# Causal attention of a decoder layer: the turn of the exponentials moved from TensorE to VectorE squares and a trip through DRAM

## The chip, the cores and the metric

The kernel runs on one core of a Trainium2 chip. All data are float32. The metric is the device time of one launch in microseconds (us); lower is better.

The core has five engines that each work through a queue of their own, in order: TensorE (PE: matmuls and transposes, results into PSUM), VectorE (DVE), ScalarE (ACT), GpSimd (POOL) and SyncE (SP), which here issues the DMAs. An engine that has to wait holds back all that is queued behind the waiting instruction.

## The reference

A decoder of two layers on x of shape [8, 128, 512] and a context of the same shape. Layer 0: causal self-attention with 32 heads of 16, an autocorrelation mixer against the context, a mixture of low-rank experts. Layer 1: causal attention with distance bias, cross-attention, low-rank experts. Each of the six blocks is followed by a residual addition and a layer norm. The change touches the first block alone:

```python
q = (x @ Wq.T + bq).reshape(b, l, h, hd).transpose(0, 2, 1, 3)      # k, v alike
scores = jnp.einsum('bhqd,bhkd->bhqk', q, k) / math.sqrt(hd)
scores = jnp.where(causal, scores, -jnp.inf)
att = jax.nn.softmax(scores, axis=-1)
out = jnp.einsum('bhqk,bhkd->bhqd', att, v)
out = out.transpose(0, 2, 1, 3).reshape(b, l, d)
return out @ Wo.T + bo
x = _layernorm(x + attention(x))
```

## The kernel before, in words

The batch is taken in pairs of sequences p = 0..3. For each pair there are four steps f = 0..3, and a step handles 8 heads of both sequences: 16 steps n = 0..15 in all (loop at L513). Where a step number stands in brackets below, it is that step's tile.

One step is an object of class `Heads16` (L146). Its work, in order:

- Scores (L165): 32 small matmuls into two PSUM tiles of two banks each. Rows are queries, columns are keys: per head pair r = 0..3, 384 columns, which are the keys of two heads for the late half of the queries (256 columns) and for the early half (128 columns).
- `causal_bias` (L369): VectorE adds the mask and writes tile `e`, [128, 4, 384], in two halves. Tile `e` has two buffers.
- Maxima (L182): four VectorE reductions.
- `exps` (L194): 16 ScalarE activations in two halves of 8, each with its sum, in place on `e`.
- `turn` (L210): VectorE takes the reciprocals `rc` of the sums (L215), GpSimd spreads them to 256 columns in `rb` (L218), TensorE transposes the 12 blocks of `e` (L225) and the two of `rb` (L233) into PSUM, VectorE and ScalarE copy the halves of `e` out to `pT` (L226), ScalarE copies the reciprocals to `rT` (L235).
- `out` (L237): 48 small matmuls of the values with `pT` (L244, L250), and one VectorE multiplication by `rT` into `oT` (L258).

The steps are staggered by the loop. In step n it issues: scores, bias, maxima and the first half of the exponentials of step n; `out` of step n-2; the queries and keys of step n+1 (L350: eight matmuls `pq` and `pk`, `qT` copied by ScalarE at L354, `kbd` made by VectorE at L358); `turn` of step n-1; pieces of the autocorrelation block (`auto`, L532 and L541, from step 7 on, for the first two pairs); values (L347) or output projections with their norms (`projection`, L371; residual addition L103) in some steps; the second half of the exponentials of step n.

That is the order in which the program is written. A scheduling layer then fixes each engine's own order when the program is built, so an instruction may stand earlier or later on its queue than the source has it. Buffers are taken from pools: a tile's next user waits until the last reader of that buffer is done. The score tiles and the transposes share one PSUM pool of two tiles (`ps2`), so the scores of a step and the transposes of another wait for each other's copies.

The weights, tokens and context are loaded at the start by some 30 DMAs on SP's queue (L300 to L338), 14 MB up to 40 us; a few later loads stand behind them.

In the last block (cross-attention, L917) the kernel already turns exponentials by VectorE in squares of 32 by 32 (`nc.vector.transpose`, L958) and moves the squares with small DMAs from SBUF to SBUF (L964). The class `Heads16` also serves the fourth block (layer 1), where the division is done ahead of the turn; that use is as it was after the change.

Of the kernel before, what the change touches and what calls it, by code (L numbers as in the profile page):

```python
# [11 lines left out]
F32 = mybir.dt.float32  # L12
AF = mybir.ActivationFunctionType
ALU = mybir.AluOpType
AX = mybir.AxisListType
PSUM = bass.MemoryType.PSUM

P = 128
B, S, D = 8, 128, 512
NC = D // P  # L20
H, HD = 32, 16
# [17 lines left out]
def bc(ap, shape):  # L39
    return ap.to_broadcast(shape)  # L40
# [3 lines left out]
def decoder(ctx: ExitStack, tc: tile.TileContext, a: dict, out: bass.AP):  # L44
    nc = tc.nc
# [4 lines left out]
    sm = ctx.enter_context(tc.tile_pool(name="sm", bufs=4))  # L50
# [28 lines left out]
    causal = masks[:, C_CAUSAL : C_CAUSAL + 3 * P]  # L79
# [66 lines left out]
    class Heads16:  # L146
# [11 lines left out]
        def __init__(self, pool, units, bias, o_dst, name, between=()):  # L158
            self.pool, self.units, self.o_dst, self.name, self.rc = pool, units, o_dst, name, None
            s = [banks(f"s_{name}_{i}") for i in range(2)]  # L160
            for part, cols, keys in ((0, slice(0, 2 * P), P), (1, slice(2 * P, 3 * P), 64)):
                for r in range(4):
                    rows = slice(32 * r, 32 * r + 32)
                    for u, (qT, kbd, _, _) in enumerate(units):
                        nc.tensor.matmul(  # L165
                            s[r // 2][64 * u : 64 * u + 64, r % 2, cols],
                            lhsT=qT[rows, 64 - 64 * part : P - 64 * part], rhs=kbd[rows, :, :keys],
                            start=True, stop=True,
                        )
            self.e = pool.tile([P, 4, self.W], F32, tag="e", name=f"e_{name}", bufs=2)  # L170
            self.m = sm.tile([P, 2, 4, 2], F32, tag="m", name=f"m_{name}")
            self.su = sm.tile([P, 2, 4, 2], F32, tag="su_a", name=f"su_{name}")
            for i in range(2):
                rs = slice(2 * i, 2 * i + 2)
                self.scored = bias(self.e[:, rs, :], s[i][:, :, : self.W], rs)

                while i and between:
                    with tc.issue_after(self.scored.ins):
                        self.scored = between.pop(0)()
                with tc.issue_after(self.scored.ins):  # L180
                    for part in range(2):
                        self.scored = nc.vector.tensor_reduce(  # L182
                            self.m[:, part, rs, :], self.by_heads(part)[:, rs], AX.X, ALU.max, negate=True
                        )

        def by_heads(self, part):
            return self.e[:, :, 2 * P * part : 2 * P + P * part].rearrange("p r (x k) -> p r x k", x=2)
# [22 lines left out]
        def turn(self):  # L210


            if self.rc is None:
                rc = sm.tile([P, 16], F32, tag="rc", name=f"rc_{self.name}")
                nc.vector.reciprocal(rc, self.su.rearrange("p a r x -> p (a r x)"))  # L215

                rb = self.pool.tile([P, 2, 8, HD], F32, tag="rb", name=f"rb_{self.name}", bufs=1)
                nc.gpsimd.tensor_copy(rb, bc(rc.rearrange("p (a h) -> p a h", a=2).unsqueeze(3), [P, 2, 8, HD]))  # L218
            self.pT = self.pool.tile([P, 4, self.W], F32, tag="pT", name=f"pT_{self.name}", bufs=1)
            for i in range(2):  # L220
                pt = banks(f"pt_{self.name}_{i}")
                for r in range(2):
                    for k in range(3):
                        cols = slice(k * P, (k + 1) * P)
                        nc.tensor.transpose(pt[:, r, cols], self.e[:, 2 * i + r, cols], ident)  # L225
                (nc.scalar.copy if i else nc.vector.tensor_copy)(  # L226
                    self.pT[:, 2 * i : 2 * i + 2, :], pt[:, :, : self.W]
                )
            if self.rc is not None:
                return  # L230
            pr = bank(f"pr_{self.name}")
            for a in range(2):
                nc.tensor.transpose(pr[:, a * P : (a + 1) * P], rb[:, a].rearrange("p h d -> p (h d)"), ident)  # L233
            self.rT = self.pool.tile([P, 2, P], F32, tag="rT", name=f"rT_{self.name}", bufs=1)
            nc.scalar.copy(self.rT, pr[:, : 2 * P].rearrange("p (a q) -> p a q", a=2))  # L235

        def out(self):  # L237
            o = bank(f"o_{self.name}")
            for u, (_, _, v, vd) in enumerate(self.units):
                v, vd = (t() if callable(t) else t for t in (v, vd))  # L240
                late = slice(u * P + 64, u * P + P)
                for x in range(2):
                    for r in range(4):
                        nc.tensor.matmul(  # L244
                            o[32 * r : 32 * r + 32, late],
                            lhsT=v[:, 48 * r + 16 * x : 48 * r + 16 * x + 32],
                            rhs=self.pT[:, r, x * P + 64 * u : x * P + 64 * u + 64], start=(x == 0), stop=(x == 1),
                        )
                for r in range(4):
                    nc.tensor.matmul(  # L250
                        o[32 * r : 32 * r + 32, u * P : u * P + 64],
                        lhsT=vd[:, 32 * r : 32 * r + 32],
                        rhs=self.pT[:, r, 2 * P + 64 * u : 2 * P + 64 * u + 64], start=True, stop=True,
                    )
            if self.rc is not None:
                nc.vector.tensor_copy(self.o_dst, o[:, : 2 * P].rearrange("p (u q) -> p u q", u=2))
                return
            nc.vector.tensor_tensor(  # L258
                self.o_dst.rearrange("p u (a q) -> p u a q", a=2),
                o[:, : 2 * P].rearrange("p (u a q) -> p u a q", u=2, a=2),  # L260
                self.rT[:, ::-1].rearrange("p a (u q) -> p u a q", u=2),
                ALU.mult,
            )

# [20 lines left out]
    ap = attn.enter_context(stage("a0", 2))  # L285
# [1 line left out]
    bq4 = ap.tile([P, NC], F32, tag="bq4", name="bq4", bufs=1)  # L287
    dft = cp.tile([P, N_DFT], F32, tag="dft", name="dft")

    idle = ap.tile([P, 4, 3 * P], F32, tag="e", name="idle").rearrange("p r k -> p (r k)")[:, :512]  # L290
    nc.vector.memset(idle, 0.0)
    nobody = bank("nobody")
    for _ in range(2):
# [56 lines left out]
    def queries_keys(p, f):  # L350
# [14 lines left out]
        )  # L365
        return qT, kbd

    def causal_bias(e, s, r0):
        return nc.vector.tensor_tensor(e, s, bc(causal.unsqueeze(1), [P, 2, 3 * P]), ALU.add)  # L369

    def projection(b, oT):  # L371
        po = bank(f"po0_{b}")
# [121 lines left out]
    steps = [(p, f) for p in range(NP) for f in range(NC)]  # L494
# [12 lines left out]
    oTs = []  # L507
# [5 lines left out]
    for n, (p, f) in enumerate(steps):  # L513
        if f == 0:
            oTs.append(ap.tile([P, 2, NC, P], F32, tag="oT", name=f"oT0_{p}"))
        qT, kbd = qk
        units = []
        for j in range(2):
            toks = slice(j * P, (j + 1) * P)
            of = lambda i, w, p=p, f=f, j=j: vs[p, j][i].rearrange("p a x d -> p (a x d)")[:, f * w : (f + 1) * w]  # L520
            units.append((qT[:, toks], kbd[:, :, toks], lambda of=of: of(0, 192), lambda of=of: of(1, 128)))
        now = Heads16(ap, units, causal_bias, oTs[p][:, :, f, :], f"a0_{p}_{f}")
        now.exps(0)
        catch_up(now.scored)

        if turned:
            turned.out()
        if n + 1 < len(steps):
            qk = queries_keys(*steps[n + 1])
        if prev:  # L530
            prev.turn()
        auto(n, 0)  # L532

        for made in values_at.get(n, ()):
            values(*made)
        now.exps(1)
        if 0 < f < 3 and p:
            projection(2 * p - 3 + f, oTs[p - 1])
        if f == 1 and p and p + 1 < NP:
            xts.append(tokens(p + 1))  # L540
        auto(n, 1)  # L541
        if n >= begun and f == NC - 1:
            context(n // NC)
        turned, prev = prev, now
# [222 lines left out]
    ap = layer.enter_context(stage("a1", 2))  # L767
# [18 lines left out]
    class Front:  # L786
# [27 lines left out]
        def begin(self):  # L814
            self.kT = cross[1].tile([P, NS, 2, 2 * P], F32, tag="kT", name=f"kTx_{self.pr}")
            self.qT = cross[1].tile([P, NX, 2 * P], F32, tag="qT", name=f"qTx_{self.pr}")
# [27 lines left out]
    for b in range(B):  # L844
# [3 lines left out]
        for f in (0, 2):  # L848
            units = []
# [3 lines left out]
            now = Heads16(ap, units, alibi_bias(f), oT[:, f : f + 2, :], f"a1_{b}_{f}", keys_late)  # L853
# [53 lines left out]
    with stage("x1b", 2, side="right") as ap, stage("f1", 2, side="right") as fp:  # L907
# [204 lines left out]
        for b in range(B):  # L1112
# [4 lines left out]
            for hh in range(2):  # L1117
                now = Heads8(front.qT[:, :, toks], front.kT[:, :, :, toks], 2 * hh, f"x1_{b}_{hh}")
# [94 lines left out]
        for half, cols in enumerate(halves):  # L1213
            po = bank(f"pox_{b}_{half}")
            for i in range(NX):
                n, h = divmod(i, G)
# [17 lines left out]
        with tc.issue_after(products.done.ins):  # L1234
            idle = banks("nobody_1")
# [159 lines left out]
```

## Time and profile before

| | |
|---|---|
| time, three runs | 882.34, 884.58, 886.21 us; median 884.58 |
| profiled execution: span, first to last instruction | 879.8 us |
| what lies around the span, by the median | 884.58 - 879.8 = 4.8 us |
| TensorE busy | 851.7 us (97%) |
| VectorE busy | 565.8 us (64%) |
| ScalarE busy | 369.5 us (42%) |
| GpSimd busy | 189.7 us (22%) |
| first attention: scores of step 0 to scores of step 15 | 10.7 to 201.2 us |
| granted TensorE clock, mean | 0.998 |

The profile is that of one execution. Its page lists busy time by engine, the span in 40 slices, the DMA queues, the chain of work that ended last, the costliest groups of instructions and the DMA issues. The timeline of an engine lists its instructions in order of time, merged where they are alike; behind them in brackets is the idle time of the engine just before, and who ended it. A start-to-start distance in a timeline is what an instruction costs its engine in a row of its kind; the listed duration is a little longer, because the next one begins while the last one drains. Matmul counts in the trace are passes: a float32 matmul shows as two.

### The profile page before, as it was taken

How to read it: one execution, taken by the hardware profiler on the slowest of the kernel's cores; microseconds unless marked ns; L12 is line 12 of the kernel's file. 1: busy time of each engine (PE TensorE's matmuls, PEld its weight loads, DVE VectorE, ACT ScalarE, POOL GpSimd, SP SyncE). 2: the span in 40 equal slices, each digit the busy share in tenths (PEclk: the TensorE clock that was granted, in tenths of full speed). 3: DMA queues.
4: the chain of work that ended last, by engine and by line, in shares of the span. 5: the costliest groups of instructions: out<-in, count | busy, mean ns of one | idle time of the engine just before them, and what ended most of it. 6: DMA issues, size and time to landing. Idle time of an engine off the chain costs nothing.

```text
span 879.8 us, 17025 instructions
## 1 busy us (share of the span) xinstructions
PE 851.7 (97%) x6482; PEld 529.6 (60%) x6482; DVE 565.8 (64%) x1334; ACT 369.5 (42%) x1535; POOL 189.7 (22%) x267
## 2 busy tenths in 40 slices
PE   9999989999899999999999999999999999999996
PEld 5766655655445555555555687758475846576454
DVE  3756797786878657888888612725363545467654
ACT  3787475565222216666666603313122322224310
POOL 2400233232243224555555300000000000000000
PEclk9999999999999999999999999999999999999999
DMA  9700000130300002000004020331113211313340
GB/s 331 303 2 25 2 13 13 49 108 3 144 12 25 1 0 91 8 1 2 2 2 145 27 72 1 76 90 43 43 36 91 44 46 37 83 42 76 84 97 36
DMA packets 30066, 50.68 MB, mean 58 GB/s; under 512 B 5536, under 2 KB 22048, under 8 KB 28192
## 3 DMA queue, kind: packets, MB, share of 16 engines
q1 hardware_dynamic: 27424, 47.49, 18.3%
q10 hardware_dynamic: 2560, 2.10, 1.1%
q8 instruction: 51, 0.84, 0.4%
q14 instruction: 31, 0.25, 0.1%
HBM read 30.69 MB, written 2.10 MB: 37 GB/s over the span
## 4 chain that ended last, share of the span: by engine, by line
PE 62%; DVE 22%; ACT 12%; issue 2%; POOL 2%; DMA 1%; SPq 0%; ACTq 0%; POOLq 0%; DVEq 0%
PE pqx L86 10%; ACT e_a L194 8%; PE pox L991 7%; PE pkx L86 4%; PE pvx L86 4%; PE s_x L929 4%; PE o_x L974 4%; PE pq L86 4%; PE pk L86 3%; DVE e_a L715 3%; PE pv L86 3%; DVE m_a L182 3%; PE pof L615 2%; PE pt_a L225 2%; PE s_a L165 2%
## 5 line engine op out<-in xcount | busy, mean ns | idle before, releaser
L194 ACT ACTIVATE e_a<-e_a,m_a 128x128 f32<-128x128 f32 (+1 forms) x512 | 184.8, 364 | 94.4 <-DVE m_a L182 94.4
L950 ACT ACTIVATE e_x<-s_x,m_x 128x256 f32<-128x256 f32 x128 | 58.6, 483 | 139.6 <-DVE m_x L940 130.9
L194 ACT ACTIVATION_READ_ACCUMULATOR e_a<-e_a,m_a 128x1 f32 x512 | 97.2, 190 | 0.0
L86 PE MATMUL pqx<-xTx,w_X_q 128*128 128x256 f32 x384 | 84.9, 380 | 0.0
L86 PEld LDWEIGHTS pqx<-xTx,w_X_q 128*128 128x128 f32 x384 | 72.7, 190 | 11.3 <-issue 1.8
L991 PE MATMUL pox<-w_X_o,oTx 128*128 128x512 f32 x168 | 74.1, 597 | 0.7 <-DVE oTx L980 0.6
L939 DVE TENSOR_REDUCE m_x<-s_x 128x4 f32<-128x1024 f32 x32 | 37.6, 1217 | 41.2 <-PE s_x L929 41.2
L182 DVE TENSOR_REDUCE m_a<-e_a 128x4 f32<-128x512 f32 (+1 forms) x128 | 62.6, 542 | 0.0
L97 POOL TENSOR_TENSOR rs_x<-ve_x,neghalf 128x1 f32<-128x1 f32 x7 | 3.8, 548 | 268.8 <-DVE ve_x L95 249.8
L208 POOL TENSOR_TENSOR e_a<-e_a,rc_a 128x512 f32<-128x512 f32 x64 | 52.6, 845 | 17.2 <-DVE rc_a L205 16.6
L991 PEld LDWEIGHTS pox<-w_X_o,oTx 128*128 128x128 f32 x168 | 31.3, 190 | 40.9 <-issue 39.1
L225 PE MATMUL pt_a<-ident,e_a 128*128 128x128 f32 x384 | 48.6, 274 | 4.5 <-DVE e_a L369 3.9
L929 PE MATMUL s_x<-kTx,qTx 32*128 32x256 f32 x768 | 50.0, 385 | 1.0 <-ACT e_x L950 1.0
L225 PEld LDWEIGHTS pt_a<-ident,e_a 128*128 128x128 f32 x384 | 43.5, 141 | 12.3 <-DVE e_a L369 4.9
L929 PEld LDWEIGHTS s_x<-kTx,qTx 32*128 32x128 f32 x768 | 39.1, 185 | 17.0 <-issue 11.7
L974 PE MATMUL o_x<-pT_x,vx 128*32 128x512 f32 x384 | 43.7, 595 | 1.8 <-issue 0.6
L958 DVE STREAM_TRANSPOSE e_x<-e_x 128x1024 f32<-128x1024 f32 x32 | 39.7, 1241 | 0.8
L957 DVE TENSOR_SCALAR e_x<-e_x,rc_x 128x256 f32<-128x256 f32 x128 | 36.3, 347 | 3.8 <-DVE rc_x L954 2.6
L103 DVE TENSOR_TENSOR x_x<-pox,x_a 128x512 f32<-128x512 f32 x7 | 4.8, 686 | 52.5 <-PE pox L991 52.5
L165 PEld LDWEIGHTS s_a<-kbd,qT 32*64 32x64 f32 x1024 | 20.7, 131 | 28.5 <-issue 12.7
L835 ACT COPY qTx<-pqx 128x512 f32<-128x512 f32 x24 | 14.1, 594 | 55.6 <-PE pqx L86 55.6
L165 PE MATMUL s_a<-kbd,qT 32*64 32x256 f32 (+1 forms) x1024 | 33.2, 335 | 2.1 <-DVE pT_a L226 1.1
(236 smaller groups left out, 1635.7 us busy)
## 6 DMA issues: line engine op xcount, KB each, us to landing
pT_x<-e_x SPq DMA_DIRECT2D x224, 64.0 KB, 2.0
w_X_q<-in_X_q SPq DMA_DIRECT2D x3, 1024.0 KB, 4.8
w_X_o<-in_X_o SPq DMA_DIRECT2D x3, 1024.0 KB, 4.8
w_L_Wv<-in_L_Wv SPq DMA_DIRECT2D x2, 1024.0 KB, 6.3
w_L_Wo<-in_L_Wo SPq DMA_DIRECT2D x2, 1024.0 KB, 7.6
x_in<-in_x SPq DMA_DIRECT2D x8, 256.0 KB, 8.2
ct<-in_ctx SPq DMA_DIRECT2D x8, 256.0 KB, 2.7
cT<-in_ctxT SPq DMA_DIRECT2D x4, 512.0 KB, 3.9
```

The costliest lines, as they stand in the source:

```text
L86: nc.tensor.matmul(ps, lhsT=l, rhs=r, start=(i == 0), stop=(i == n - 1))
L165: nc.tensor.matmul(s[r // 2][64 * u : 64 * u + 64, r % 2, cols], lhsT=qT[rows, 64 - 64 * part : P - 64 * part], rhs=kbd[rows, :, :keys], s ...
L182: self.scored = nc.vector.tensor_reduce(self.m[:, part, rs, :], self.by_heads(part)[:, rs], AX.X, ALU.max, negate=True)
L194: nc.scalar.activation(e[:, r, x, :], e[:, r, x, :], AF.Exp, bias=self.m[:, part, r, x : x + 1], accum_out=self.su[:, part, r, x : x + 1],)
L208: nc.gpsimd.tensor_tensor(e, e, bc(self.rc[:, part, rs, :].unsqueeze(3), list(e.shape)), ALU.mult)
L225: nc.tensor.transpose(pt[:, r, cols], self.e[:, 2 * i + r, cols], ident)
L929: nc.tensor.matmul(sc[g // 2][:, g % 2, u * 256 : (u + 1) * 256], lhsT=qT[rows, (h0 + u) * NS + n, :], rhs=kT[rows, n], start=(n == 0), st ...
L939: nc.vector.tensor_reduce(m, self.s[i], AX.X, ALU.max, negate=True)
L950: nc.scalar.activation(self.e[:, :, j, :], self.s[half][:, i, :].rearrange("p (a k) -> p a k", k=32), AF.Exp, bias=self.m[:, j : j + 1], s ...
L958: nc.vector.transpose(self.e[:, :, js, :], self.e[:, :, js, :])
L974: nc.tensor.matmul(po[32 * g : 32 * g + 32, :], lhsT=v[:, s, g * XD + 32 * n : g * XD + 32 * n + 32], rhs=pT[:, s].rearrange("p i h x -> p ...
L991: nc.tensor.matmul(po, lhsT=oT[:, n, h * P : (h + 1) * P], rhs=w, start=(i == 0), stop=(i == NX - 1))
```

## The change

Fifteen of the 16 steps use a new class, `Squares16`; the last step uses `Divided16`, which turns on TensorE as before (its reciprocals and results lie behind those of `e` and `pT` in one tile, rather than in tiles of their own).

In `Squares16` the tile `e` is laid out by squares: [128, 4, 14, 32], four groups of 32 keys, 12 columns of squares for the exponentials and two for the spread reciprocals. Bias, maxima and exponentials address it by squares. After the second half of a step's exponentials `move` follows at once: reciprocals on VectorE, their spreading on GpSimd into the last two columns of `e`, two VectorE transposes in squares (1536 and 256 columns, in place), and one DMA of the whole tile (128 x 1792, 896 KB) into a DRAM tile `kept` with three buffers. In the place of the old `turn`, one step later, four DMAs of 32 partitions (224 KB each) read the DRAM tile back into `pT`, with partition and group exchanged; `pT` has one buffer and now holds the turned reciprocals too. `out` reads `pT` by squares, and the final multiplication takes the reciprocals from `pT`. The 14 TensorE transposes, the two copies of `pT` and the copy of `rT` go in these steps.

```diff
+    class Squares16(Heads16):
+        keys = AX.XY
+        def begin(self):
+            self.e4 = self.pool.tile([P, 4, 14, 32], F32, tag="e", name=f"e_{self.name}", bufs=2)
+            self.e = self.e4[:, :, :12, :].rearrange("p g (r t) k -> p r t g k", r=4)
...
+        def move(self):
+            rc = sm.tile([P, 16], F32, tag="rc", name=f"rc_{self.name}")
+            nc.vector.reciprocal(rc, self.sums.rearrange("p r a x -> p (r a x)"))
+            nc.gpsimd.tensor_copy(
+                self.e4[:, :, 12:14, :].rearrange("p g a (x d) -> p g (a x) d", x=2),
+                bc(rc.rearrange("p (r h) -> p r h", r=4).unsqueeze(3), [P, 4, 4, HD]),
+            )
+            for rows in (slice(0, 12), slice(12, 14)):
+                nc.vector.transpose(self.e4[:, :, rows, :], self.e4[:, :, rows, :])
+            self.kept = kept_rows.tile([P, 4, 14 * 32], F32, tag="kept", name=f"kept_{self.name}")
+            nc.sync.dma_start(self.kept, self.e4.rearrange("p g r k -> p g (r k)"))
+        def turn(self):
+            self.pT = self.pool.tile([P, 4, 14, 32], F32, tag="pT", name=f"pT_{self.name}", bufs=1)
+            by_group = self.kept.rearrange("(i k) g x -> k i g x", i=4)
+            to = self.pT.rearrange("p i r k -> p i (r k)")
+            for g in range(4):
+                nc.sync.dma_start(to[32 * g : 32 * g + 32], by_group[:, :, g, :])
+        def probabilities(self, r, t, u):
+            return self.pT[:, 2 * u : 2 * u + 2, 3 * r + t, :]
+        def divided(self, o):
+            by_half = "p u (a i q) -> p a u i q"
+            rT = self.pT[:, :, 12:14, :].rearrange("p (u i) a q -> p a u i q", u=2)
+            nc.vector.tensor_tensor(
+                self.o_dst.rearrange(by_half, a=2, i=2),
+                o[:, : 2 * P].rearrange("p (u t) -> p u t", u=2).rearrange(by_half, a=2, i=2),
+                rT[:, ::-1],
+                ALU.mult,
+            )
...
+    kept_rows = ctx.enter_context(tc.tile_pool(name="kept", bufs=3, space=bass.MemoryType.DRAM))
...
     def causal_bias(e, s, r0):
-        return nc.vector.tensor_tensor(e, s, bc(causal.unsqueeze(1), [P, 2, 3 * P]), ALU.add)
+        by_squares = causal.rearrange("p (t g k) -> p t g k", t=3, g=4).unsqueeze(1)
+        return nc.vector.tensor_tensor(e, s, bc(by_squares, [P, 2, 3, 4, 32]), ALU.add)
...
-        now = Heads16(ap, units, causal_bias, oTs[p][:, :, f, :], f"a0_{p}_{f}")
+        kind = Squares16 if n + 1 < len(steps) else Divided16
+        now = kind(ap, units, causal_bias, oTs[p][:, :, f, :], f"a0_{p}_{f}")
...
         now.exps(1)
+        if n + 1 < len(steps):
+            now.move()
```

## The prediction, made before the changed kernel was run

> **What bounds the kernel now.** I read the page first, then the chain, then the timelines of TensorE and VectorE for one step, then DMA.
>
> ```profile
> PE 851.7 (97%) x6482; PEld 529.6 (60%) x6482; DVE 565.8 (64%) x1334; ACT 369.5 (42%) x1535; POOL 189.7 (22%) x267
> ...
> PE 62%; DVE 22%; ACT 12%; issue 2%; POOL 2%; DMA 1%; SPq 0%; ACTq 0%; POOLq 0%; DVEq 0%
> ```
>
> TensorE is busy almost always, but only 62% of the chain is its own: elsewhere it would soon run out of work if VectorE or ScalarE came later. So a stage has two limits close together. In the first attention I write B(n) for the start of step n's bias on VectorE. Step 5, from the timelines of TensorE and VectorE:
>
> ```profile
> 56.60 0.91 PE L165 MATMUL s_a<-kbd,qT 32*64 32x256 f32 x32
> ...
> 58.25 2.00 PE L86 MATMUL pq<-xT,w_L_Wq 128*128 128x256 f32 x8
> 60.08 1.89 PE L86 MATMUL pk<-xT,w_L_Wk 128*128 128x256 f32 x8
> 61.81 1.47 PE L225 MATMUL pt_a<-ident,e_a 128*128 128x128 f32 x12
> 63.12 0.38 PE L233 MATMUL pr_a<-ident,rb_a 128*128 128x128 f32 x2
> 63.33 3.60 PE L86 MATMUL po<-w_L_Wo,oT 128*128 128x512 f32 x8
> 66.86 0.91 PE L165 MATMUL s_a<-kbd,qT 32*64 32x256 f32 x32
> ```
>
> ```profile
> 57.65 1.81 DVE L369 TENSOR_TENSOR e_a<-s_a,masks 128x768 f32<-128x768 f32 x2
> 59.38 1.92 DVE L182 TENSOR_REDUCE m_a<-e_a 128x4 f32<-128x512 f32 x4
> ...
> 67.41 0.25 DVE L215 RECIPROCAL rc_a<-su_a 128x16 f32<-128x16 f32 x1 [3.79 <-ACT e_a L194]
> 67.58 0.63 DVE L103 TENSOR_TENSOR x_a<-po,x_in 128x512 f32<-128x512 f32 x1
> 68.12 0.94 DVE L369 TENSOR_TENSOR e_a<-s_a,masks 128x768 f32<-128x768 f32 x1
> ```
>
> The reader should see two rings of nearly equal length. TensorE goes round in 10.26 us without a gap. VectorE idles 3.79 us for the last exponential, takes the reciprocal and only then begins the next bias: B(5) to B(6) is 10.47. So this step is a ring of bias, maxima, exponentials, reciprocal, next bias, too; TensorE is hardly ahead of it. The ring is broken in some steps: rc(1) and rc(3) stand behind the next bias, at 32.53 and 51.08, and those periods are short (21.7 to 28.6, 39.0 to 47.2).
>
> **What goes.** Per step TensorE loses 14 transposes, 61.81 to 63.33 above: 1.53 us start to start; 15 steps: 23 us. VectorE loses one copy of 0.88 (L226), ScalarE two copies, 0.69 + 0.26 = 0.95 (L226, L235), and the short waits for PSUM, 0.3 to 0.6.
>
> **What comes.** The nearest VectorE row for the squares is in the cross-attention:
>
> ```profile
> L958 DVE STREAM_TRANSPOSE e_x<-e_x 128x1024 f32<-128x1024 f32 x32 | 39.7, 1241 | 0.8
> ```
>
> 1241 ns for 1024 columns; the new ones have 1536 and 256. Bounds for the long one: one such row (1.2) and two (2.5); by length 1.75. The short one: 0.35 (a 256-column reduction is 0.41). Together 2.1 us a step. Bias by squares of 32: the 16x2x16 form of L347 takes 0.67 for 512 columns, the plain L103 0.67 too, so nothing; exponentials by squares: L950, which writes 8x32, takes 483 ns for 256 columns against 456 for the plain L354, so 0 to 0.03 each, 0 to 0.4 a step; I take 0.
>
> What decides is where they stand. VectorE's order of the changed program (read from the built program, no time in it) has reciprocal(n), both transposes(n), and then bias(n+1), in **all** 15 steps. The transposes need the second half of the exponentials, so VectorE waits for ScalarE in every step with bias(n+1), and often kbd(n+1), values and norms behind it. That is a new wait: queued behind are the next bias and so ScalarE's next exponentials. The ring becomes: B to first exponential 2.5 (39.04 to 41.53); 16 exponentials with the query copy in between 6.1 (95.33 to 102.38 less the two copies), or 5.75 where the copy is outside; to the reciprocal 0.13; reciprocal 0.17; transposes 2.1. Sum **11.0** (10.7 with the copy outside). TensorE without transposes needs 10.26 - 1.53 = 8.7 in a step with a projection or values and 5.2 in one without, so from step 1 to 7 it waits, and its saving is off the path.
>
> Step by step, from B(0) = 11.6:
> - B(1): reciprocal 19.9, transposes and the values queued between them: 22.8. B(2): 22.8 + 10.7 = 33.5 (before: 28.6).
> - B(3) waits for the start-up: out(0) needs the round trip through DRAM. Its write is issued at 25.8 at the earliest, when SP is through the loads, and queues behind them. The load issued last (25.4) took 13.4 us to land, at 38.8, by the list of DMA issues:
>
> ```profile
> w_L_Wk<-in_L_Wk SPq DMA_DIRECT2D x1, 1024.0 KB, 13.4
> ```
>
>  The write of 896 KB then needs about 2.2 at the 420 GB/s of the early windows: 41; reads follow, behind the write of step 1, four issues 0.6 apart (L964 takes 595 ns) and 2.7 to land (256 KB context loads): 46. TensorE's queue holds everything behind out(0): then out(0) 0.8, queries and keys 3.6, values 3.5, scores 0.9 give B(3) = 54.9. Without this wait it would be 33.5 + 10.7 + multiplication 0.3, kbd 0.7, scores 0.9 = 46.1; so 8.8 us are on the path.
> - B(4) = 54.9 + 11.0 = 65.9. B(5) = 65.9 + 10.7 + 0.3 (multiplication) + 1.6 (kbd, then the scores that need it, both now behind the transposes) = 78.5. B(6) = 78.5 + 11.0 + 0.6 (x addition) = 90.1. B(7) = 90.1 + 10.7 + 1.6 = 102.4. Before: 47.2, 57.7, 68.1, 78.5. Deficit at step 7: 23.9.
> - B(8) = 102.4 + 11.0 + two spectra products 2.3 + values 0.6 = 116.3 (before 92.8).
> - Steps 8 to 15: autocorrelation pieces stand behind the transposes on VectorE. Maxima, 4.8 (103.41 to 108.25): 15.9. Then, where the products wait for ScalarE's copies of the turned weights behind the exponentials: exponentials end 8.4, weights, matmuls and copies 4.5, last product 1.2, x 0.6, hops: 15.3. Then norm 1.9, additions 1.2, products 2.3: 16.4. Then norm pieces, products and values 4.2: 15.2. Then the first three again: 110.4 for the seven. Before: 15.4, 15.1, 16.2, 15.9, 15.4, 15.1, 16.2, together 109.3. B(15) = 226.7 against 202.1.
> - The last step keeps TensorE's transposes; ScalarE has no older copies to do: 1.0 back.
>
> Sum: 24.6 - 1.0 = **23.6**. Of this 8.8 is the start-up, the rest the ring.
>
> **Round trips after the start.** Write 896 KB: between 2.2 (256 KB output) and 4.8 (1 MB loads alone); I take 4.5. Read: 3 x 0.6 + 2.7 = 4.5 to 5. About 9.5 from the end of the transposes. out(n) comes after the scores of n+2, one ring plus 1.5 to 2.6 later, 12 to 13. pT has one buffer and waits for the multiplication of the step before; that stands late in steps 4 and 5, behind reciprocal or maxima, and leaves 0 to 2 us of slack. So it is hidden, narrowly. SP's other loads (tokens, context, weights) now stand between these DMAs; each waits for a reader that comes sooner. GpSimd's spreading (0.40) hides beside the long transpose.
>
> **The clock.** TensorE will idle some 17 us before out(0) and 5 us before the scores of steps 5 and 7.
>
> ```profile
> 1.45 3.78 PE L294 MATMUL nobody<-idle 128*128 128x512 f32 x4 [1.45 <-DVE idle L291]
> ```
>
> ```profile
> 875.00:880.00 5.00, 0.00 (x0) 0.00 (x0) 1.27 (x4) 0.00 (x0) 0.72 (x1) 0.63 0.28 105
> ```
>
> The first matmuls took 3.78 for what takes 1.88 later (poc, L86, x4), and in the last 5 us of the span, in a stretch without a matmul, the mean granted clock was 0.63. So idling can cost speed. Bounds: 0, and at half speed 2 of the work behind out(0) and the scores of steps 5 and 7 doubled (0.8 each), 3.6; I take 3, as the idle is long. Total 23.6 + 3 = 26.6.
>
> The span of 879.8 becomes 906.4; with 4.8 around it (the profiled execution has no time of its own beside the span; 4.8 is the median of the three runs, 884.58, less the span) **911 us**.
>
> A rule on this point: the Trainium skill, VectorE: DVE Perf Modes, section Rules for kernel authors, says to turn 128x128 on TensorE where PSUM will do and to use VectorE for 32x32; its section The three transpose paths gives 390 ns for TensorE and 311 for VectorE. The trace has 109 ns (1.31/12) and 155 (1241/8) in float32. By the page's prices 15 x 14 x 390 ns = 82 us of TensorE would go, and the rival of a bound TensorE would give about 803; the rows decide.
>
> **The rivals.**
> 1. *The ring and the start-up* (forecast): 911, by the sum; with transposes at 1.2 or 2.5 it runs from 903 to 922. For it: the 3.79 wait above in front of the reciprocal. Chance 0.52.
> 2. *The ring without the start-up*: the write of step 0 does not queue behind the loads, or out(0) costs no path. 911 - 8.8 - 2 = 900. Against it: 13.4 us of landing at 25.4. Chance 0.16.
> 3. *The round trip ends last too*: transfers take 7 us each (1 MB loads took 6.3 to 7.6 in median when not alone), 14 against 12 to 13; with the buffer of pT about 2.5 late in four steps: 921. Chance 0.17.
> 4. *TensorE stays the bound* (faster): the ring would have to fit within TensorE's round, which needs the transposes to leave VectorE's path, below a ring of 8.7 in the early steps. 15 x 1.53 = 23: 861. For it: 97% busy. It decides the sign if exponentials end before VectorE gets to the reciprocal; the 2.8 to 3.8 idle there says the contrary. Chance 0.08.
> 5. *It evens out*: early loss given back by late steps where TensorE sets the pace: 885. Chance 0.03. The transposes do leave the program, so it does what it says; other slower ways 0.04.
>
> **Numbers.** Faster 0.08, same 0.03, slower 0.89, with 0.5% (4.4 us) as about what a measurement can tell. The range leaves out 4, 5 and the ends: 897 to 924.
>
> **What would show it.** Right: the reciprocal waits for ScalarE in every step, B to B near 11 in steps 3 to 7; TensorE waits at out(0) for a DMA until about 46; scores in steps 5 and 7 wait for kbd; clock below 1 around there; the stage after it as before, only later. Wrong: reciprocals without idle time in front of them; out(n) waiting for a DMA in many steps (rival 3); TensorE without gaps (rival 4).

## The result, and the profile after

The changed kernel takes 929.27 us (median of 4 runs, 927.95 to 931.17) against 883.7 us of the kernel before beside it: ratio 1.052, 95% interval 1.0495 to 1.0545. Forecast were 911 us, 897 to 924. The direction was right, the size was not: 45.6 us were added where 26.6 were expected. All of it lies in the first attention: from the first projection of the last pair of batches (po, below "end") to the last instruction it is 662.7 us before and 663.1 after.

The page of the changed kernel, with the busy time by engine, the granted clock by slice and the chain:

```profile
PE 848.0 (92%) x6272; PEld 516.8 (56%) x6272; DVE 583.4 (63%) x1349; ACT 356.0 (38%) x1505; POOL 188.4 (20%) x267
...
PEclk9687899998889999999999999999999999999999
...
PE 52%; DVE 25%; ACT 12%; DMA 4%; issue 3%; POOL 2%; SPq 0%; ACTq 0%; POOLq 0%; DVEq 0%
```

TensorE is busy for 3.7 us less, though 23 us of transposes are gone; its clock is no longer full in the first third; DMA now has 4% of the chain. The changed kernel by stages of the first attention (length, busy times, granted clock, DMA):

```profile
10.80:58.50 47.70, 26.53 (x243) 17.18 (x242) 21.87 (x35) 18.94 (x99) 12.65 (x16) 0.75 0.86 313
58.50:109.70 51.20, 36.64 (x408) 25.11 (x408) 30.82 (x51) 25.01 (x132) 3.61 (x9) 0.84 0.54 153
109.70:202.00 92.30, 83.48 (x722) 47.52 (x722) 70.99 (x155) 46.87 (x212) 21.17 (x28) 0.96 0.43 125
202.00:263.60 61.60, 48.69 (x456) 27.32 (x455) 45.27 (x117) 27.93 (x113) 13.69 (x18) 0.83 0.48 146
```

The first busy column is TensorE: 26.53 of 47.70 us, then 36.64 of 51.20. Steps 5 and 6 on TensorE and VectorE, which answer to the timelines of step 5 before:

```profile
81.75 1.59 PE L165 MATMUL s_a<-kbd,qT 32*64 32x256 f32 x32 [4.93 <-DVE kbd L440]
86.05 0.66 PE L260 MATMUL o_a<-pT_a,v 128*32 128x64 f32 x14 [2.71 <-DMA pT_a<-kept_a]
...
87.60 3.01 PE L86 MATMUL pq<-xT,w_L_Wq 128*128 128x256 f32 x8
90.44 1.89 PE L86 MATMUL pk<-xT,w_L_Wk 128*128 128x256 f32 x8
92.17 3.60 PE L86 MATMUL po<-w_L_Wo,oT 128*128 128x512 f32 x8
95.70 0.91 PE L165 MATMUL s_a<-kbd,qT 32*64 32x256 f32 x32
```

```profile
83.36 1.82 DVE L454 TENSOR_TENSOR e_a<-s_a,masks 128x768 f32<-128x768 f32 x2 [1.16 <-PE s_a L165]
...
92.37 0.75 DVE L440 SCALAR_TENSOR_TENSOR kbd<-pk,vecs,masks 128x512 f32<-128x512 f32 x1 [4.23 <-PE pk L86]
93.04 0.24 DVE L317 RECIPROCAL rc_a<-su_a 128x16 f32<-128x16 f32 x1
93.20 2.04 DVE L323 STREAM_TRANSPOSE e_a<-e_a 128x1536 f32<-128x1536 f32 x2
...
96.64 0.96 DVE L454 TENSOR_TENSOR e_a<-s_a,masks 128x768 f32<-128x768 f32 x1
```

The transposes take 2.04 us, as sized. But here VectorE waits 4.23 us for a key projection, not for ScalarE, and TensorE waits 2.71 us for the read-back. The start, on TensorE and on VectorE, and the landing times of the round trip:

```profile
47.39 0.66 PE L260 MATMUL o_a<-pT_a,v 128*32 128x64 f32 x16 [19.30 <-DMA pT_a<-kept_a]
...
48.83 3.61 PE L86 MATMUL pq<-xT,w_L_Wq 128*128 128x256 f32 x8
```

```profile
41.06 1.82 DVE L454 TENSOR_TENSOR e_a<-s_a,masks 128x768 f32<-128x768 f32 x2 [7.82 <-DMA kept_a<-e_a]
```

```profile
kept_a<-e_a SPq DMA_DIRECT2D x15, 896.0 KB, 4.5
pT_a<-kept_a SPq DMA_DIRECT2D x60, 224.0 KB, 4.3
```

out(0) waits 19.3 us and starts at 47.4 (46 was forecast). The bias of step 2 waits for the write of step 0 to leave its buffer, which the forecast did not have. A read takes 4.3 us in the median to land from its issue, and the four issues of a step stretch over 1.73 us; for the multiplication at 86.05 above the first is at 78.98 and the last lands at 85.91, 6.9 us. From the timelines, in us, B(n) being the start of step n's bias:

| | B(3) | B(3) to B(8) | B(8) to end | end |
|---|---|---|---|---|
| before | 39.04 | 53.8 | 124.3 | 217.15 |
| forecast | 54.9 | 61.4 | 124.4 | 240.7 |
| changed | 58.48 | 68.3 | 136.8 | 263.57 |

So 3.6 us were missed in the start, 6.9 in the early steps and 12.4 in the late ones. (The forecast's row does not hold its 3 us for the clock, which it added to the sum at the end.) By steps, the early 6.9 are 0.4, 0.9, 1.7, 0.8 and 3.1 us in steps 3 to 7. The late 12.4 are 6.8 in steps 8 to 14 (117.2 us for 110.4) and 5.6 in the last step (19.6 for 14.0). Two waits stand out there. In step 7 the autocorrelation's first matmuls wait for the bias, ahead of the second multiplication:

```profile
110.72 1.11 PE L480 MATMUL pa<-x_a,dft 128*64 128x512 f32 x1 [1.04 <-DVE e_a L454]
...
114.84 0.43 PE L260 MATMUL o_a<-pT_a,v 128*32 128x64 f32 x16
```

In the last step the multiplication of step 14 waits for its read:

```profile
255.15 0.65 PE L260 MATMUL o_a<-pT_a,v 128*32 128x64 f32 x16 [2.25 <-DMA pT_a<-kept_a]
```

### The profile page after: what moved, and what is told of

Its sections match the earlier page's. It is cut to its first block, busy times and chain, and to the rows that moved or that the text cites. A ratio compares the mean times of both kernels' runs of the same rounds, so it can differ in the third digit from the quotient of the medians.

```text
span 926.7 us, 16763 instructions
## 1 busy us (share of the span) xinstructions
PE 848.0 (92%) x6272; PEld 516.8 (56%) x6272; DVE 583.4 (63%) x1349; ACT 356.0 (38%) x1505; POOL 188.4 (20%) x267
## 4 chain that ended last, share of the span: by engine, by line
PE 52%; DVE 25%; ACT 12%; DMA 4%; issue 3%; POOL 2%; SPq 0%; ACTq 0%; POOLq 0%; DVEq 0%
ACT e_a L207 9%; PE pqx L86 9%; PE pox L1079 6%; PE pvx L86 4%; PE s_x L1017 4%; PE pkx L86 4%; PE o_x L1062 4%; DVE e_a L803 3%; PE pq L86 3%; DVE m_a L181 3%; PE pof L703 2%; DVE e_a L454 2%; PE pk L86 2%; DMA pT_a<-kept_a 2%; DVE e_a L323 2%
## 5 line engine op out<-in xcount | busy, mean ns | idle before, releaser
L86 PEld LDWEIGHTS pqx<-xTx,w_X_q 128*128 128x128 f32 x384 | 72.6, 190 | 11.4 <-issue 1.8
L260 PE MATMUL o_a<-pT_a,v 128*32 128x64 f32 x1024 | 27.5, 236 | 26.9 <-DMA pT_a<-kept_a 24.3
L165 PE MATMUL s_a<-kbd,qT 32*64 32x128 f32 (+1 forms) x1024 | 35.5, 347 | 13.4 <-DVE kbd L440 11.3
L260 PEld LDWEIGHTS o_a<-pT_a,v 128*32 128x32 f32 x1024 | 20.6, 118 | 39.6 <-issue 39.1
L86 PE MATMUL pq<-xT,w_L_Wq 128*128 128x256 f32 x128 | 37.1, 439 | 1.0 <-DMA xT<-in_xT 1.0
```

The costliest lines, as they stand in the source:

```text
L86: nc.tensor.matmul(ps, lhsT=l, rhs=r, start=(i == 0), stop=(i == n - 1))
L165: nc.tensor.matmul(s[r // 2][64 * u : 64 * u + 64, r % 2, cols], lhsT=qT[rows, 64 - 64 * part : P - 64 * part], rhs=kbd[rows, :, :keys], s ...
L260: nc.tensor.matmul(o[32 * r : 32 * r + 32, late], lhsT=v[:, 48 * r + 16 * x : 48 * r + 16 * x + 32], rhs=self.probabilities(r, x, u), star ...
```

## The experiments

**Theory S**: what I missed belongs to the round trip through DRAM (its start, its read buffer, the order that it brings). **Theory R**, the forecast's own emphasis: VectorE's ring with the transposes in it sets the pace. Each run below states two rival theories of its own ahead of its result. Times are medians; the kernel before took 882.5 to 883.8 beside them. Where an edit changes which steps are `Squares16`, the condition ahead of `now.move()` changes with it.

**1. First steps on TensorE.**

```
-        kind = Squares16 if n + 1 < len(steps) else Divided16
+        kind = Squares16 if 2 < n < len(steps) - 1 else Divided16
```

> Steps 0 to 2 are turned on TensorE as before the change, steps 3 to 14 in squares through DRAM. Theory S (the time that I missed lies in the round trip's start: the write of step 0 stands behind the loads, holds an exponential buffer until 41.0 us and out(0) until 47.4 us): the bias of step 3 comes back to about 39 to 40 us from 58.5, and nearly all of these 19 us are kept to the end: 929 - 19 = 910 us, 906 to 914. Rival A (what is lost at the start would be lost later anyway, to late loads or to the autocorrelation): 920 us or more.

909.65 us. B(3) is 39.08, the end 244.22, 19.35 earlier than in the change: theory S. Steps 3 to 8 still take 67.1, the rest 138.1.

**2. No transposes on VectorE.**

```
-            for rows in (slice(0, 12), slice(12, 14)):
-                nc.vector.transpose(self.e4[:, :, rows, :], self.e4[:, :, rows, :])
```

> The two transposes on VectorE are left out, the write and the read through DRAM stay; the output is computed from probabilities that are not turned. Theory R (VectorE's ring from one bias to the next sets the step wherever no transfer does): 2.04 us of 11 to 18 us a step go in 10 to 15 steps, so 20 to 31 us: 898 to 909 us. Rival T (transfers, score banks and the clock set the steps, so that VectorE's time is mostly slack): less than 10 us: 919 us or more.

920.38 us: 8.9 less, theory T. The transposes themselves are a small part of the 45.6.

**3. No round trip.**

```
-            nc.sync.dma_start(self.kept, ...)       # kept and its tile
...
-                nc.sync.dma_start(to[32 * g : 32 * g + 32], by_group[:, :, g, :])
+            self.pT = still[0]                      # set once by nc.gpsimd.memset
```

> The round trip is left out: the transposes on VectorE stay, nothing is written to DRAM or read back, and the second multiplication reads a tile that GpSimd fills once with a constant (the output is computed from that constant). Theory S (the time I missed is the round trip's: its start, the single read buffer, the cold clock after waits): what is left is the ring alone, which the prediction priced at 900 us; 893 to 905 us. Rival R (the ring of VectorE and the banks behind it carry the loss, the trip little): 915 us or more.

883.54 us, ratio 1.0015 (1.0000 to 1.0029): below theory S's range, equal to the kernel before. So in this program the reciprocals, the transposes and the squares cost nothing. But this run leaves out more than the transfers. Its second multiplication reads a constant and waits for no turn, and the program was built with other orders: the whole bias of steps 2 and 5, and the first half of that of steps 3 and 6, stand ahead of the transposes of the step before. Step 5:

```profile
55.79 1.82 DVE L450 TENSOR_TENSOR e_a<-s_a,masks 128x768 f32<-128x768 f32 x2 [0.48 <-PE s_a L165]
...
58.79 0.25 DVE L317 RECIPROCAL rc_a<-su_a 128x16 f32<-128x16 f32 x1 [1.18 <-ACT e_a L207]
58.96 2.04 DVE L323 STREAM_TRANSPOSE e_a<-e_a 128x1536 f32<-128x1536 f32 x2
```

So the ring of the forecast is broken in four of the first rounds here, and the run does not show what an unbroken ring costs. It shows that the loss needs the trip, or the waits and orders that come with it.

**4. ScalarE's queue for the first three steps.**

```
-            nc.sync.dma_start(self.kept, ...)       # and the four reads
+            self.queue().dma_start(self.kept, ...)  # nc.scalar in steps 0 to 2
```

> The write and the four reads of steps 0, 1 and 2 are issued on ScalarE's queue instead of SyncE's. Theory Q (the order within one queue kept the first write behind the loads): it lands about 6 us after its issue at 26 us, the bias of step 2 starts near 33.5 us instead of 41.1, out(0) before 40 us instead of 47.4: 8 to 12 us less, 917 to 921 us. Rival B (all queues share the same DMA engines, which the loads fill until about 44 us): landing times stay, 926 to 932 us.

933.51 us. Its chain:

```profile
23.12 7.02 DMA kept_a<-e_a
...
31.55 15.42 DMA pT_a<-kept_a
...
47.18 0.65 PE o_a L260 x16
```

That is above both ranges and 4.2 us slower than the change; which wait adds these was not tried. The write lands in 7.0 us, and B(2) is 30.2 instead of 41.1. But it did not pass the loads: three of the last four were issued only at 30.2 to 31.0, after it had landed, where the change issued them at 24.1 to 25.4, ahead of its write. The read, issued from 30.2 to 31.5 beside these three, took 15.4 us, and out(0) starts at 47.2 as before. So rival B for the read. And the exponential buffer that the write held, which I had suspected from the 7.82 us above, was not on the path to out(0).

**5. Only the late steps in squares.**

```
-        kind = Squares16 if n + 1 < len(steps) else Divided16
+        kind = Squares16 if 7 < n < len(steps) - 1 else Divided16
```

> Steps 0 to 7 are turned on TensorE as before the change, only steps 8 to 14 in squares through DRAM as the change has it. In the changed kernel the stretch from the bias of step 8 to the end of the stage is 136.8 us where it was 124.3 before. Theory L (the late steps lose these 12.5 us by themselves, through matmuls that wait for score banks and for the last reads): the bias of step 8 is back near 93 us and the kernel comes to 893 to 899 us. Rival C (the late loss only follows the disturbed start, and TensorE's saved transposes come through without it): 876 to 887 us.

896.41 us, theory L: B(8) is 93.0, the rest 135.3. The late loss is its own, and comes without any disturbed start.

**6 and 7. The move behind the next bias**, in steps 8 to 14, and in all.

```
+        if 8 < n:                        # 7: if prev:
+            with tc.issue_after(now.scored.ins):
+                prev.move()
         now.exps(0)
...
-            now.move()                   # behind exps(1)
```

> As the run that turns only steps 8 to 14 in squares, but the reciprocal, the transposes and the write of a step are issued behind the bias and the maxima of the next step. Theory V (in the late steps it is the place of the transposes ahead of the next bias that keeps score banks and so TensorE; the round trip has room in steps of 15 us): 7 x 1.53 = 10.7 us of TensorE's transposes come back, 873 to 884 us. Rival T (the round trip, begun about 5 us later, now lands behind the multiplication that reads it, 2 to 4 us a step): 893 us or more.

> The change with the reciprocal, the transposes and the write of every step issued behind the bias and the maxima of the next step; nothing else differs. Theory T (the round trip is what costs: in the early steps of about 10.5 us it now begins 5 to 6 us later and lands about 16.7 us after the next bias, behind the multiplication): slower than the change, 932 to 955 us. Rival R (the ring through VectorE is what costs, and this cuts it): faster than the change, 915 us or less.

907.93 and 937.97 us: theory T both times. Moving the transposes behind the next bias makes it slower, as the transfer then begins later; in the first, TensorE waits 12.8 us for read-backs, three times, up to 6.8.

**8 and 9. A clock kept full.** Filling matmuls ahead of out(0).

```
+        if n == 2:
+            warm = bank("warm")
+            for _ in range(66):          # 9: range(42)
+                nc.tensor.matmul(warm[:, : 2 * P], lhsT=masks[:, :P], rhs=masks[:, : 2 * P], start=True, stop=True)
         if turned:
             turned.out()
```

> The change, with 66 matmuls (128x128 by 128x256) of a constant table, into a bank that nobody reads, ahead of the first multiplication that waits for the read-back, so that TensorE stays busy for most of the 19.3 us in which it waits there. Theory K (the clock that follows the gap costs: the first query projection after it took 3.61 us where it took 2.0 before): the projections after it come back to about 2 us, the bias of step 3 starts 2.5 to 4 us earlier, 924 to 927 us. Rival N (the clock after that gap is hidden by later waits): 928 to 931 us.

934.83 us. I had mis-sized the filling: one matmul is two passes of 0.218 us, so it ran until 55.4 and held up out(0) by 8 us. Nothing follows for the clock from its time.

> The change with 42 filling matmuls ahead of the first multiplication instead of 66: one of them took 0.436 us, so that they end near 45.0 us, ahead of the 47.4 us at which the read lands, and TensorE idles about 2.4 us there instead of 19.3. Theory K (the clock falls to half in that gap and stays there for about 5 us of work behind it): the bias of step 3 starts at 55 to 56 us instead of 58.5, 925.5 to 927.5 us. Rival N (later waits take it up): 928.5 to 931 us.

929.53 us: rival N. The clock's part worked: by stretch (clock third from the end), the change first, then this run,

```profile
28.00:32.00 4.00, 0.09 (x8) 0.00 (x0) 0.96 (x2) 3.01 (x18) 3.93 (x4) 0.53 1.01 416
...
48.00:52.00 4.00, 4.00 (x43) 3.21 (x36) 2.48 (x4) 1.49 (x10) 0.40 (x1) 0.50 0.02 4
52.00:56.00 4.00, 4.00 (x15) 2.73 (x14) 0.79 (x2) 0.47 (x1) 0.00 (x0) 0.98 0.84 252
```

```profile
48.00:52.00 4.00, 4.00 (x28) 3.34 (x18) 2.52 (x5) 1.92 (x11) 0.40 (x1) 1.00 0.00 0
...
56.00:60.00 4.00, 0.07 (x8) 0.00 (x0) 3.66 (x6) 1.30 (x7) 0.80 (x2) 1.00 1.09 240
```

the query projection is back at 1.99 us and B(3) at 56.12 instead of 58.48. Then TensorE stands still from 56 to 60, waiting for the next read-back, and B(4) is 71.08, later than the change's 69.91. In this new gap the clock falls again (mean 0.51 from 60 to 64, the next query projection 3.78 us). So what the filling gives back is lost to the next transfer, and the slow clock moves on with it. What a full clock throughout would be worth, no run shows.

**10 and 11. TensorE's order.** The late steps show this, first on TensorE, then on VectorE, step 9 of the change:

```profile
138.24 0.91 PE L165 MATMUL s_a<-kbd,qT 32*64 32x256 f32 x32
143.43 2.95 PE L542 MATMUL pvf<-ct,dft 128*128 128x512 f32 x4 [4.28 <-DVE e_a L454]
```

```profile
135.67 2.04 DVE L323 STREAM_TRANSPOSE e_a<-e_a 128x1536 f32<-128x1536 f32 x2
137.63 0.45 DVE L517 MAX8 top<-co 128x8 f32<-128x128 f32 x2
...
142.23 0.28 DVE L523 MATCH_REPLACE8 wk<-nxt,wk 128x128 f32<-128x128 f32 x1
142.42 0.95 DVE L454 TENSOR_TENSOR e_a<-s_a,masks 128x768 f32<-128x768 f32 x1
```

The autocorrelation's pvf needs a pair of score banks that the bias frees; the bias stands behind the transposes and the autocorrelation's maxima. Before, the same VectorE work stood there, but on TensorE the scores were followed by

```profile
105.15 0.43 PE L244 MATMUL o_a<-pT_a,v 128*32 128x64 f32 x16
...
105.95 2.00 PE L86 MATMUL pq<-xT,w_L_Wq 128*128 128x256 f32 x8
107.78 1.89 PE L86 MATMUL pk<-xT,w_L_Wk 128*128 128x256 f32 x8
109.51 0.82 PE L225 MATMUL pt_a<-ident,e_a 128*128 128x128 f32 x6
112.29 0.88 PE L225 MATMUL pt_a<-ident,e_a 128*128 128x128 f32 x6 [1.96 <-DVE e_a L369]
```

work that needs no bias, six of the transposes among it (the other six wait 1.96 us). In the changed build pvf stands ahead of the second multiplication, whose input now comes from DRAM. (In run 3, where it does not, pvf stands behind the key projection; that the input is the reason is an inference.) The edit puts it back, once for the late steps alone and once in the whole change:

```
-        auto(n, 0)
+        with tc.issue_after(queries_keys.done.ins):   # the last key matmul
+            auto(n, 0)
```

> As the run that turns only steps 8 to 14 in squares (896.4 us), but the autocorrelation's matmuls of a step's first place are kept behind the key projection in the order of TensorE, where they stood before the change, instead of ahead of the second multiplication. Theory O (the late loss is this order: such matmuls wait for score banks that the bias frees, 4.3, 6.1 and about 1 us a time, and the bias stands behind the autocorrelation's own VectorE work): the 12.5 us come back, 880 to 886 us. Rival D (the round trip itself is late in these steps, and the order only shows it elsewhere): 892 to 898 us.

> The whole change with the same order: the autocorrelation's matmuls behind the key projection of the step. Theory O: 10 to 13 us less than the change, 916 to 920 us, with the bias of step 8 still near 126.7 us. Rival D: 926 to 932 us.

889.59 us (6.8 less than run 5) falls between the two theories; 918.98 us is theory O: 10.3 less than the change by the medians, 7.0 at the end of the stage in the profiled executions (the profiled one of this run is its slowest, 922.14 us). Of these 7.0 step 7 gives 2.7 (14.3 us for 17.0) and steps 8 to 14 give 4.6 (112.6 for 117.2); the last step is as long as in the change. TensorE in step 9 of the second:

```profile
135.96 1.99 PE L86 MATMUL pq<-xT,w_L_Wq 128*128 128x256 f32 x8
137.79 1.89 PE L86 MATMUL pk<-xT,w_L_Wk 128*128 128x256 f32 x8
144.13 0.86 PE L130 MATMUL pt_wT<-ident,ex 128*128 128x128 f32 x4 [4.46 <-POOL ex L533]
```

The projections now fill the time, and a different wait follows: for the autocorrelation's weights, 9.5 us in three pieces, 8.7 of them in this stage (before 1.3, all behind it). They come later, with the transposes ahead of the maxima on VectorE. But run 3 has the same wait (9.8 us, 8.4 in this stage), and from B(8) to the end it takes 122.4 us, less than the kernel before. So this wait takes back what TensorE saves; it does not account for the loss that is left.

**12. A read buffer that is free sooner.**

```
+            self.rq = self.pool.tile([P, 4, 2, 32], F32, tag="rq", ..., bufs=1)
+            nc.gpsimd.tensor_copy(self.rq, self.pT[:, :, 12:14, :])   # divided() reads rq
```

> The change, with GpSimd copying the turned reciprocals out of the read buffer, so that the next read no longer waits for VectorE's multiplication but for TensorE's second multiplication and that copy. Theory B (the single read buffer, held by a multiplication that stands behind the reciprocal on VectorE, makes the reads of steps 3, 5 and 14 late): 3 to 7 us less than the change, 922 to 926 us. Rival N (the reads have room or wait for their writes anyway): 927 to 932 us.

922.30 us, theory B: 7.0 less. The read of step 3 is issued at 73.2 instead of 79.0, the next at 84.0 instead of 88.2. But the early steps keep little of it: B(3) to B(8) is 66.9 for 68.3 (step 5 is 1.8 us shorter, step 7 longer by 1.4). Most of it lies in the last step, 16.1 us for 19.6, where the wait of 2.25 us is gone.

**13 and 14. All mends together** (the edits of 1, 11 and 12), then with the write behind the read of the step before on SyncE's queue.

> The three mends at once: steps 0 to 2 turned on TensorE, the autocorrelation's matmuls behind the key projection, the reciprocals copied out of the read buffer. Theory A (three separate losses): 929.3 less 19.6, 10.3 and 7.0 gives 892.4 us, 889 to 896 us. Rival O (they overlap: one wait was counted under several names): 899 us or more.

901.46 us: the overlap rival. The trace shows a wait that run 1 had too; SyncE's queue and TensorE:

```profile
60.44 10.89 SPq L326 DMA_DIRECT2D kept_a<-e_a  x2
71.62 12.24 SPq L333 DMA_DIRECT2D pT_a<-kept_a  x8
```

```profile
80.54 0.65 PE L261 MATMUL o_a<-pT_a,v 128*32 128x64 f32 x16 [7.29 <-DMA pT_a<-kept_a]
```

The write of step 5 waits in SyncE's queue for the transposes, and the read of step 4 behind it.

```
+            with tc.issue_after(Squares16.read.ins) if Squares16.read else nullcontext():
                 nc.sync.dma_start(self.kept, ...)
```

> As the run with three mends (901.5 us), but the write of a step stands behind the read of the step before it on SyncE's queue. Theory Q (in steps 4 to 6 of that run the read of step 4 waited 7.3 us behind the write of step 5, which waits for VectorE's transposes; the queue's order hid what the free read buffer gives): the multiplication of step 4 no longer waits, 892 to 896 us, which is what the three mends added up to. Rival O (the losses overlap, whatever the order): 898 to 903 us.

892.26 us, theory Q; the read of step 4 is issued at 69.7. B(3) to B(8) is 62.0, the rest 126.4. It equals the sum of runs 1, 12 and 11, but four things are mended, not three: the bad queue order was already inside run 1. How much each would give alone stays open to that extent. Of the 9.2 us that still stand against the kernel before, 8.2 are from B(3) to B(8) and 2.1 behind it, by the profile. TensorE still waits in the first two steps that use the trip:

```profile
61.45 0.65 PE L261 MATMUL o_a<-pT_a,v 128*32 128x64 f32 x16 [4.88 <-DMA pT_a<-kept_a]
...
76.66 0.66 PE L261 MATMUL o_a<-pT_a,v 128*32 128x64 f32 x16 [3.51 <-issue]
```

The second wait has no releaser in the trace, but it ends as GpSimd's copy of the same read begins (76.7), and the read was issued from 69.7 on. So even with its buffer and its queue mended the trip is longer than its cover in steps of 8 to 14 us; that these two waits are what is left is read from the trace, not tried.

**15 and 16. Squares only where TensorE was busy throughout** (on top of the edits of 11 and 12), then with TensorE's transposes held behind the key projection too.

```
+        kind = Squares16 if n in (7, 10, 11) else Divided16
...
+            with tc.issue_after(queries_keys.done.ins) if not isinstance(prev, Squares16) else nullcontext():
                 prev.turn()                      # 16 only
```

> Squares through DRAM only in steps 7, 10 and 11, whose transposes on TensorE fall in steps 8, 11 and 12, where TensorE was busy for the whole step before the change; the other steps on TensorE, with the order and the read buffer mended. Theory G (where TensorE has no idle time and VectorE has, a step's 1.53 us come off): 878 to 882 us, faster than before. Rival N (VectorE's order or the round trip takes the gain in these steps too): 883 to 887 us or more.

> As the run with squares in steps 7, 10 and 11 only (887.2 us), but TensorE's transposes of the other steps are kept behind the key projection, where they stood before the change; in that run they stood ahead of the second multiplication of steps 7 and 11 and waited 5.1 and 5.2 us for the bias, against 1.96 us each before. Theory G (with the order restored the saved 3 x 1.53 us come off): 877 to 882 us. Rival N (the time goes to another wait): 883 to 888 us.

887.17 us (1.0059, 1.0037 to 1.0081) and 886.20 us (1.0040, 1.0026 to 1.0054): rival N twice. No version here beats the kernel before. In the last one TensorE waits, in step 9:

```profile
111.96 0.87 PE L239 MATMUL pt_a<-ident,e_a 128*128 128x128 f32 x6 [1.57 <-DVE e_a L457]
...
117.42 3.16 PE L545 MATMUL pvf<-ct,dft 128*128 128x512 f32 x4 [3.93 <-DVE pT_a L240]
```

Steps 8, 11 and 12 together are 2.1 us shorter than before, step 9 is 3.5 us longer: what TensorE saved there it waits for VectorE here.

## Why the prediction was right in direction and wrong in size

- **The start-up** ("so 8.8 us are on the path"): right in kind, short in size. out(0) came at 47.4 for 46. The other 2.2 us that are missing at B(3) are mostly the half clock behind the gap (query projection 3.61 for 2.0; run 9 brings B(3) 2.4 us forward, and loses them to the next read); for this the forecast had its 3 us in the sum. Run 1 returns 19.6 us by taking the first steps off the trip.
- **"So it is hidden, narrowly"**: this step failed. The read was sized at 4.5 to 5 us from the tail of 256 KB loads; it took 6.9 where it is shown above. The four issues were as sized (1.73 us for 1.8); the landing was not, 5.6 us for 2.7. The single buffer that I gave 0 to 2 us of slack had none in steps 5 and 15: run 12 returns 7.0 us, by its profile 1.8 in step 5 and 3.5 in the last step. Rival 3 (921 us) had this mechanism, for four steps; it was too cheap.
- **"Steps 8 to 15 ... 110.4 for the seven. Before ... 109.3"**: this step failed too. The seven took 117.2. I followed VectorE's order piece by piece and let TensorE run on. TensorE's order had changed as well: work without need of a bias was gone or moved back, and a matmul that waits for score banks stood in its place. Run 5 shows that the late steps lose time without any disturbed start; run 11 puts TensorE's order back and returns 4.6 us in these steps and 2.7 in step 7, where 3.1 were missed. The 2.2 us that stay missing in these steps are not explained.
- **The ring of 11.0**: its parts were right (transposes 2.04 for 2.1; the reciprocal waits 4.79 us for ScalarE in step 4), B(3) to B(4) is 11.4. As a price it was probably too high: leaving the transposes out returns 8.9 us (run 2), and without the trip the kernel is as fast as before (run 3), where rival 2's ring alone gave 900. But run 3's program breaks the ring in four of its rounds, so the price of the unbroken ring stays open. What is shown is the weight of the other term, which I had as nearly hidden: the mends of the trip and of TensorE's order return 37 of the 45.6 us (run 14).
- **TensorE's saving off the path**: right, and more than forecast. Runs 15 and 16 find no place where it stays as a gain.
- **The clock, 3 us**: the cause was there (mean 0.961). The same 6272 passes keep TensorE busy for 848.0 us in the change and for 836.1 without the trip:

```profile
PE 836.1 (95%) x6272; PEld 510.1 (58%) x6272; DVE 579.9 (66%) x1349; ACT 356.1 (40%) x1505; POOL 190.0 (22%) x268
...
PEclk9999989999999999999999999999999999999998
```

 These are 11.9 us more of busy time for the same passes, at a mean clock of 0.961 for 0.990, but not that much of the total: run 9 mends one such gap and gains nothing, as the next wait takes its place.
- **The last step, 1.0 back**: wrong sign. It is 4.6 us longer than before (19.6 for 15.0); the multiplication of step 14 waits 2.25 us for its read, behind the single buffer, and run 12 returns 3.5 of it.

The Trainium skill, TensorE: Matmul & The Clock Gate, Part 1: The HAM clock gate, has the clock at half after about one idle window of 3.4 us, and full again after about as long of sustained work. The rows agree in the half (0.50). The rise differs from place to place: work resumes at 47.4 and the clock is full from 52.1, 4.7 us later; it is 3.6 us behind the wait of 2.71 us (86.05 to 89.7), and 6.1 us in run 9 (60.8 to 66.9).

## What to carry to other kernels

When work leaves the engine that is busiest, read that engine's new order as carefully as the order of the engine that takes the work: what stood behind the removed instructions moves up, and it may wait for something that they covered. A trip through memory counts from the last producer to the last landing, with its place in the queue, the issues, and whoever holds its buffer; where only 1 us of cover is left, it is to be priced as not hidden. And two runs that leave out one half of a change each (here 920 and 884 us) point at the half to price again, as far as the engines' orders stayed the same; in the second of these they did not.

## What the runs showed of the hardware

- A second issuing queue moved the loss rather than ending it (run 4). The write issued at 23.1 on ScalarE's queue landed in 7.0 us, and SyncE's queue issued three loads of 1 MB only behind it, at 30.2 to 31.0. The read issued on ScalarE's queue beside them landed 15.4 us after its last issue, and the last of the three loads took as long. The Trainium skill, DMA: Bandwidth & Descriptors, section Issuing engines are not separate DMA queues, says that issuing engines share the DMA engines; the read agrees with that.
- The granted clock changed on a grid. In the change's profile it falls at 28.25, 62.38, 79.45 and 106.76 us and rises at 52.14, 65.80, 89.69 and 113.58 (from windows of 0.1 us, between 28 and 114 us). All of these lie whole multiples of 3.41 us apart: 7, 3, 1, 4, 3, 5 and 2 of them from one to the next. So what a gap did to the clock depended on where it fell. Behind the last matmul at 76.8 the clock fell after 2.6 us, behind that at 56.1 in run 9 after 4.0, and the gap of 2.4 us at 58.4 in the change was over when the clock fell at 62.38, under running matmuls. Filling a gap with matmuls that nobody reads kept the clock at 1.00 (run 9, 28 to 48 us).
